# Tap matrices in runs of six pixels of one group, in two involution layers

## The chip, the cores and the metric

The kernel runs on one core of a Trainium2 chip. The metric is the device time of one execution in microseconds, the median over several runs. The core has five engines with instruction streams of their own: PE multiplies matrices and writes to PSUM, DVE and ACT read PSUM and SBUF, POOL reads SBUF alone, and SP issues DMA transfers. They wait for one another by semaphores. All arithmetic is in fp32.

## The reference

Four residual layers work on `x`, of 4 images with 256 channels of 56 x 56 pixels. Each layer normalises its input by groups of eight channels and adds its result to `x`. Layers 0 and 2 are involutions: every pixel has its own 7 x 7 filter for each of 16 groups of 16 channels, computed from the pixel's own channels.

```python
# layer 0; layer 2 has a batch norm and a relu after reduce_w, and another pair behind the sum
h = jnp.einsum('bchw,oc->bohw', xk, reduce_w) + reduce_b[None, :, None, None]
kern = jnp.einsum('bchw,oc->bohw', h, span_w) + span_b[None, :, None, None]
kern = kern.reshape(b, G, 1, K * K, Ho, Wo)
out = (kern * patches).sum(axis=3)
...
x = x + _L0_conv_ref(_gn(x), ...)     # involution
x = x + _L1_conv_ref(_gn(x), ...)     # two 3 x 3 convolutions
x = x + _L2_conv_ref(_gn(x), ...)     # involution
x = x + _L3_conv_ref(_gn(x), ...)     # gates from sums over a Fourier transform
```

`h` has 64 rows. `span_w` makes of it 49 filter taps for each group.

## The kernel before

The change touches layers 0 and 2 alone, which share the function `involution_layer`. The image is cut into tiles of 3 x 8 pixels (`TY`, `TX`; 24 pixels, `TP`). 19 x 7 tiles (`NT`, 133) cover it. The window that a tile needs, with the border of the filter, has 9 x 14 pixels (`Q`, 126): the partitions of one matmul. A column of tiles (`tx`, seven of them) is the unit of the apply work.

A unit of work is one image `b` and one half `cb` of the channels, eight groups (`GB`). There are eight units in each of the two layers, counted here 0 to 7 in layer 0 and 8 to 15 in layer 2. Each has two phases.

**Tap phase.** `tap_matrices` (L582) fills `kt`, for each group and each of a tile's 24 pixels the 126 x 133 matrix of what each window pixel counts for that pixel, over all tiles. One matmul (L593) gives one pixel of one group: the stationary operand is a stretch of 126 columns of the span table `z_sb`, which holds the 49 taps of a group spread over a field of `ZN` = 161 columns with zeros between them, shifted by the pixel's place; the moving operand is `hp`, the 64 rows of `h` at that pixel of every tile. Since only 64 rows are summed over, `hp` lies twice in SBUF, on partitions 0 to 63 and 64 to 127, and two matmuls run beside each other on the two halves of the array. The table has even groups on the first half of the partitions and odd groups on the second, so a step takes three pixels (`PB`) of two groups: six matmuls into two PSUM banks. Thirty-two steps make a unit. Every third step is evacuated by ACT with six activations that add the bias (L604), the others by DVE with one operation (L611). Other work (norms, window transposes, loads) is put between the steps by `hooks`.

The layout is `kt = [Q, GB, TP // PB, NT, PB]`: in one partition a group has eight blocks of three pixels, and in a block the three pixels of one tile lie beside each other.

**Apply phase.** For each column of tiles, `apply` (L623) multiplies the windows `xw` with the tap matrices. The stationary operand is a window with the channels of four groups (64) or two groups (32), the moving operand those groups' 24 pixels of that tile out of `kt` (L635): 96 or 48 elements, read in runs of `PB`. Two or four such matmuls run beside each other on column tiles of the array. A column has 20 matmuls of the first kind and 36 of the second. ACT and DVE then pick each channel's own group out of the four or two (L648 or L650, L655), and POOL (L660) or DVE (L662) adds the result to `x` in SBUF.

The windows come by a chain of their own: a strip of the normalised image (`strip_sb`, one buffer; L391 on POOL in layer 0, L389 on ACT in layer 2), seven transposes on PE (L406), a copy out of PSUM by ACT (L418) into one of three buffers `xw`, and four DMA transfers within SBUF that move rows between partitions (L424, L426, issued by SP, one of the four in layer 0 by POOL). This runs three columns ahead.

**Order.** Every engine runs its instructions in the order in which the program issues them (`in_order`). In the column loop of L1107 a column's apply is followed by `next_windows` and `next_strip`, the sums of the column before, and the closures in `late[tx]`: the next image's bottleneck, in layer 2 the gating of the image before (`next_load`, `next_gate` on POOL), and in unit 6 the building of the table for layer 2.

**The span tables.** Layer 0's is built at the start by ACT (`begin`, L496; `span_table`, L334). Layer 2's is built by POOL in the last image of layer 0 (`tables2`, L1004), stored to DRAM with one transfer (L1014), and loaded before unit 8 (L971). PSUM is used in four double banks (`two_banks`).

Of the kernel before, what the change touches and what calls it, by code (L numbers as in the profile page):

```python
# [16 lines left out]
P = 128  # L17
# [5 lines left out]
R = 64  # L23
# [19 lines left out]
ZN = ZF + Q  # L43
PB = 3
ROWS_H = 9
# [26 lines left out]
def net_kernel(  # L72
# [44 lines left out]

    z2_dram = dram.tile([P, G // 2, ZN], F32, name="z2_dram")
    zb2_dram = dram.tile([Q, G, TP], F32, name="zb2_dram")
# [179 lines left out]
    def involution_layer(layer, xin, xout, red, span, sb, xs_of, ahead=None, pending=None):  # L299

        with ExitStack() as es:
# [24 lines left out]
            if layer == 0:  # L326
# [3 lines left out]
                nc.scalar.activation(norm_sb[:, 3, B - 1, 1, :], mhalf, AF.Sigmoid)  # L330
            z_sb = wpool.tile([P, G // 2, ZN], F32, name="z_sb")
            zb_sb = wpool.tile([Q, G, TP], F32, name="zb_sb")

            def span_table(z_sb, span, scratch, load, copy):  # L334


                taps = scratch[:, : NB * KK * KK * GB].rearrange("p (cb k g) -> p cb k g", cb=NB, g=GB)
                for i in range(2):
                    for cb in range(NB):
                        load(taps[i * R : (i + 1) * R, cb], span[cb * R : (cb + 1) * R])  # L340
                nc.gpsimd.memset(z_sb, 0.0)
                yield
                for i in range(2):
                    half = slice(i * R, (i + 1) * R)
                    for cb in range(NB):
                        m = GB // 2
                        for gp in range(m):
                            copy(
                                field(z_sb[half, cb * m + gp, :]),
                                taps[half, cb, :, 2 * gp + i].rearrange("p (y x) -> p y x", x=KK),  # L350
                            )
                            yield
# [143 lines left out]
            def begin():  # L496
# [83 lines left out]
                return folds  # L580

            def tap_matrices(b, cb, hooks):  # L582

                hp = h_of[b]
                kt = big.tile([Q, GB, TP // PB, NT, PB], F32, name="kt")
                for n in range(GB // 2 * TP // PB):
                    gp, pb = divmod(n, TP // PB)
                    ps = two_banks()
                    for k in range(PB):
                        py, px = divmod(pb * PB + k, TX)  # L590
                        z0 = ZF - py * QX - px
                        for i in range(2):
                            nc.tensor.matmul(  # L593
                                ps[:Q, i, k * NT : (k + 1) * NT],
                                z_sb[i * R : (i + 1) * R, cb * GB // 2 + gp, z0 : z0 + Q],
                                hp[i * R : (i + 1) * R, py, px].rearrange("p a t -> p (a t)"),
                                start=True,
                                stop=True,
                            )
                    g0, p0 = 2 * gp, pb * PB  # L600
                    if n % 3 == 2:
                        for i in range(2):
                            for k in range(PB):
                                nc.scalar.activation(  # L604
                                    kt[:, g0 + i, pb, :, k],
                                    ps[:Q, i, k * NT : (k + 1) * NT],
                                    AF.Identity,
                                    bias=zb_sb[:, cb * GB + g0 + i, p0 + k : p0 + k + 1],
                                )
                    else:  # L610
                        nc.vector.tensor_tensor(  # L611
                            kt[:, g0 : g0 + 2, pb],
                            ps[:Q, :, : PB * NT].rearrange("q i (k t) -> q i t k", k=PB),
                            zb_sb[:, cb * GB + g0 : cb * GB + g0 + 2, p0 : p0 + PB]
                            .unsqueeze(2)
                            .to_broadcast([Q, 2, NT, PB]),
                            ALU.add,
                        )
                    for h in hooks.get(n, ()):
                        h()  # L620
                return kt
# [347 lines left out]
            else:  # L969
                since = mark()  # L970
                nc.sync.dma_start(z_sb, z2_dram)  # L971
                nc.sync.dma_start(zb_sb, zb2_dram)
# [31 lines left out]
            def tables2():  # L1004
# [6 lines left out]
                next(biases)  # L1011
                yield from span_table(z2, span2, scratch, nc.sync.dma_start, nc.gpsimd.tensor_copy)
                next(biases)
                nc.sync.dma_start(z2_dram, z2)  # L1014
                yield

            prev = None
            for u, (b, cb) in enumerate(units):
# [70 lines left out]
                if layer == 2 and b > 0:  # L1089
                    if cb == 0:  # L1090
                        late[0] += [lambda b=b, j=j: load_sf(b - 1, j) for j in range(2)]
                    for tx in range(1, 6) if cb == 0 else range(NTX - 2):
                        late[tx] += [next_load, next_gate]
                if last_image and cb == 0:
                    for tx in range(6):
# [663 lines left out]
```

## Time and profile before

| what | value |
|---|---|
| median of 3 runs | 1796.4 us (1794.46 to 1797.01) |
| span of the profiled execution | 1791.4 us |
| granted TensorE clock, mean | 0.985 |
| a tap phase, first to last matmul, units 0 to 7 | 23.9 to 27.4 us |
| a tap phase, units 8 to 15 | 26.2 to 30.2 us |
| apply phases of units 0, 2, 4 and 6, seven columns | 28 to 29 us |
| apply phases of units 9, 11 and 13 | 34 to 36 us |
| one apply column without other work | 4.11 us |
| layer 1, the convolutions | from 513 to 1257 us |

A line of the groups reads: line of the kernel, engine, operation, tile written <- tiles read, shapes, count | busy time in us, mean ns of one | idle time of the engine just before them, and what ended it. A fp32 matmul shows as two records[...]: how fast they run is read from how far apart they start. PEld is the loading of the stationary operand. In the timeline the columns are the start in us, the length in us, the engine, the line, the operation and how many of them were merged; a bracket is idle time before it and what ended it. The page's other parts add that DVE was busy 77% of the span and the DMA engines moved 120 GB/s on average, in the last third 150 to 220.

### The profile page before, as it was taken

To read this page: it belongs to the slowest core of one execution; us is meant where nothing else is said; L and a number is where in the kernel's file an instruction comes from. 1 tells how busy PE (TensorE), PEld (TensorE's weight loads), DVE (VectorE), ACT (ScalarE), POOL (GpSimd) and SP (SyncE) were. 2 spreads that over 40 slices of the span, in tenths; PEclk is the share of its full clock that TensorE was granted. 3 is DMA by queue.
4 is the path that set the end of the run, shared out by engine and by line. 5 is a ranking of instruction groups with operands and counts; after the bars stand their busy time and mean duration, and the time that the engine had idled before them with its cause. 6 is when DMAs were issued, how large, how long until landed. Compare 5 with 4: busy or idle time off the path is not lost.

```text
span 1791.4 us, 55774 instructions
## 1 busy us (share of the span) xinstructions
PE 1716.7 (96%) x24040; PEld 1507.5 (84%) x24040; DVE 1385.3 (77%) x2745; ACT 813.5 (45%) x1882; POOL 406.2 (23%) x627
## 2 busy tenths in 40 slices
PE   6999999999999999999999999999999999999998
PEld 4998988889978988898889888986888887788886
DVE  2777787767778988988898889885777778687775
ACT  2555556555533222222323132111767667567564
POOL 2224422444320000000000000001000355463572
PEclk9999999999989999999999999999999999999997
DMA  2445444633653021211111111122344567566653
GB/s 86 135 151 170 140 146 134 196 107 119 204 171 105 32 75 51 76 33 64 58 68 44 52 63 37 44 110 73 122 164 156 162 213 220 169 223 189 183 154 115
DMA packets 66003, 215.76 MB, mean 120 GB/s; under 512 B 13237, under 2 KB 20926, under 8 KB 62046
## 3 DMA queue, kind: packets, MB, share of 16 engines
q1 hardware_dynamic: 49262, 145.37, 25.9%
q0 software_dynamic: 14656, 64.77, 11.3%
q8 instruction: 190, 3.11, 0.7%
q10 hardware_dynamic: 1840, 2.05, 0.4%
q14 instruction: 55, 0.45, 0.1%
HBM read 76.30 MB, written 49.15 MB: 70 GB/s over the span
## 4 chain that ended last, share of the span: by engine, by line
PE 68%; DVE 19%; ACT 4%; DMA 4%; issue 3%; POOL 2%; SPq 1%; POOLq 0%; ACTq 0%; DVEq 0%
PE mm L1523 17%; PE ps L593 14%; PE ps L635 14%; PE mm L1441 9%; DVE kt L611 6%; PE mm L1412 5%; PE ps L406 3%; DMA xw<-xw 3%; DVE un L655 3%; PE ps L469 1%; DVE res L1516 1%; DVE xs L1375 1%; DVE st L1105 1%; ACT kt L604 1%; ACT hp L488 1%
## 5 line engine op out<-in xcount | busy, mean ns | idle before, releaser
L635 PE MATMUL ps<-kt,xw 126*32 126x48 f32 (+1 forms) x12544 | 381.8, 235 | 27.8 <-issue 12.2
L635 PEld LDWEIGHTS ps<-kt,xw 126*32 126x32 f32 (+1 forms) x12544 | 341.9, 121 | 74.5 <-issue 45.5
L593 PE MATMUL ps<-hp,z_sb 64*126 64x133 f32 x6144 | 383.2, 279 | 8.4 <-DVE kt L611 4.6
L1523 PE MATMUL mm<-v,u_sb 128*128 128x280 f32 (+1 forms) x1728 | 383.5, 383 | 1.9 <-DVE u_sb L1254 1.5
L593 PEld LDWEIGHTS ps<-hp,z_sb 64*126 64x126 f32 x6144 | 363.6, 185 | 24.4 <-DVE kt L611 6.8
L611 DVE TENSOR_TENSOR kt<-ps,zb_sb 126x798 f32<-126x798 f32 x352 | 332.9, 980 | 60.4 <-PE ps L593 49.2
L1523 PEld LDWEIGHTS mm<-v,u_sb 128*128 128x128 f32 x1728 | 326.1, 189 | 56.3 <-DVE u_sb L1254 1.9
L604 ACT ACTIVATE kt<-ps,zb_sb 126x133 f32<-126x133 f32 x960 | 280.1, 441 | 107.3 <-PE ps L593 107.3
L1441 PE MATMUL mm<-v,u_sb 128*128 128x252 f32 (+1 forms) x936 | 209.5, 384 | 0.0
L1441 PEld LDWEIGHTS mm<-v,u_sb 128*128 128x128 f32 x936 | 176.4, 189 | 30.5 <-issue 0.8
L655 DVE SCALAR_TENSOR_TENSOR un<-ps,s,un 128x240 f32<-128x240 f32 x224 | 102.6, 458 | 86.7 <-ACT un L650 79.9
L1560 POOL DMA_DIRECT2D x<-xs x24 | 13.1, 547 | 680.1 <-DVE xs L1559 426.5
L655 DVE SCALAR_TENSOR_TENSOR un<-ps,par_sb,un 128x240 f32<-128x240 f32 x224 | 98.1, 457 | 86.8 <-ACT un L648 82.3
L1508 ACT ACTIVATE res<-xs,shift,norm_sb 128x1120 f32<-128x1120 f32 (+1 forms) x24 | 30.2, 1258 | 236.3 <-DVE xs L1559 107.3
L418 ACT COPY xw<-ps 126x896 f32<-126x896 f32 x112 | 101.2, 905 | 44.0 <-PE ps L406 38.5
L406 PE MATMUL ps<-ident_sb,strip_sb 128*126 128x128 f32 x784 | 111.9, 283 | 8.4 <-POOL strip_sb L391 5.3
L660 POOL TENSOR_TENSOR xs<-un,xs 128x240 f32<-128x240 f32 x112 | 72.1, 664 | 192.2 <-DVE un L655 192.1
L648 ACT ACTIVATE un<-ps,par_sb 128x240 f32<-128x240 f32 x112 | 50.1, 448 | 122.5 <-PE ps L635 120.6
L650 ACT ACTIVATE un<-ps,bn_t,s 128x240 f32<-128x240 f32 x112 | 60.1, 537 | 94.7 <-PE ps L635 88.7
L406 PEld LDWEIGHTS ps<-ident_sb,strip_sb 128*126 128x126 f32 x784 | 85.1, 142 | 19.5 <-POOL strip_sb L391 8.3
L1412 PE MATMUL mm<-xs,u_sb 128*128 128x126 f32 (+1 forms) x792 | 98.7, 277 | 2.3 <-DVE xs L1375 1.3
L1412 PEld LDWEIGHTS mm<-xs,u_sb 128*128 128x128 f32 x792 | 94.4, 191 | 3.7 <-DVE xs L1428 1.6
(256 smaller groups left out, 1903.1 us busy)
## 6 DMA issues: line engine op xcount, KB each, us to landing
xw<-xw SPq DMA_DIRECT2D x168, 252.0 KB
xw<-xw SPq DMA_DIRECT2D x224, 126.0 KB
xw<-xw POOLq DMA_DIRECT2D x56, 252.0 KB, 4.6
xs<-x SPq DMA_DIRECT2D x24, 560.0 KB
x<-xs POOLq DMA_DIRECT2D x8, 1568.0 KB, 7.5
xs<-x SPq DMA_DIRECT2D x8, 1568.0 KB
xs<-in_x_dram SPq DMA_DIRECT2D x6, 1568.0 KB
x<-xs SPq DMA_DIRECT2D x6, 1568.0 KB
```

Of the source, the lines that this page charges most:

```text
L406: nc.tensor.transpose(ps[:Q, k * P : (k + 1) * P], flat[:, k * Q : (k + 1) * Q], ident_sb)
L418: nc.scalar.copy(xw[:, :NSB, :], ps[:Q, : NSB * P].rearrange("q (n c) -> q n c", n=NSB))
L593: nc.tensor.matmul(ps[:Q, i, k * NT : (k + 1) * NT], z_sb[i * R : (i + 1) * R, cb * GB // 2 + gp, z0 : z0 + Q], hp[i * R : (i + 1) * R, py ...
L604: nc.scalar.activation(kt[:, g0 + i, pb, :, k], ps[:Q, i, k * NT : (k + 1) * NT], AF.Identity, bias=zb_sb[:, cb * GB + g0 + i, p0 + k : p0 ...
L611: nc.vector.tensor_tensor(kt[:, g0 : g0 + 2, pb], ps[:Q, :, : PB * NT].rearrange("q i (k t) -> q i t k", k=PB), zb_sb[:, cb * GB + g0 : cb ...
L635: nc.tensor.matmul(v[m * j : m * j + m, i, :, k * TP : (k + 1) * TP], xw[:, window(ty), m * j : m * j + m], kt[:, ng * j : ng * j + ng, :, ...
L650: nc.scalar.activation(part, o[0], AF.Identity, bias=bn["t4"][:, cb : cb + 1], scale=bn["s4"][ng][:, 0, cb : cb + 1])
L655: nc.vector.scalar_tensor_tensor(part, o[e], s, part, ALU.mult, ALU.add)
L660: nc.gpsimd.tensor_tensor(dst, u, dst, ALU.add)
L1412: nc.tensor.matmul(ps[:, co * m : (co + 1) * m], u[ci][:, co * P : (co + 1) * P], v2[:, e, : n // 2, ci * WT : (ci + 1) * WT], start=(ci = ...
L1441: nc.tensor.matmul(ps, u1_sb[:, ci, dy, k, co * P : (co + 1) * P], v[:, k, dy * NB + ci : (dy + n - 1) * NB + ci + 1 : NB, :], start=(j == 0),
L1523: nc.tensor.matmul(ps, u2_sb[:, ci, dy, k, co * P : (co + 1) * P], v[:, k, dy * NB + ci : (dy + n - 1) * NB + ci + 1 : NB, :], start=(j == 0),
```

## The change

A step of the tap phase makes six pixels of one group instead of three pixels of two groups. Both halves of the array now work on the same group, the first on pixels 0 to 2 of the six, the second on 3 to 5. So `kt` becomes `[Q, GB, 4, NT, 6]`, with the six pixels of a tile beside each other, and each group's table has to lie on both halves of the partitions. There are as many steps, matmuls, activations and DVE operations as before, with the same numbers of elements.

In layer 0 the table gets twice the columns (16 groups on all 128 partitions). In layer 2 it keeps its size and holds the eight groups of one `cb` at a time: it is loaded again for each unit, in the second column of the unit before. The stored table has all groups on both halves, written with eight transfers.

```diff
-PB = 3
+PB, PR = 6, 3
...
-    z2_dram = dram.tile([P, G // 2, ZN], F32, name="z2_dram")
+    z2_dram = dram.tile([NB, P, GB, ZN], F32, name="z2_dram")
...
-            z_sb = wpool.tile([P, G // 2, ZN], F32, name="z_sb")
+            z_sb = wpool.tile([P, G if layer == 0 else GB, ZN], F32, name="z_sb")
...
-            def span_table(z_sb, span, scratch, load, copy):
+            def span_table(z_sb, span, scratch, load, copy, halves=((slice(0, P), 1),)):
...
-                for i in range(2):
-                    half = slice(i * R, (i + 1) * R)
+                for half, by in halves:
                     for cb in range(NB):
-                        m = GB // 2
-                        for gp in range(m):
+                        m = GB // by
+                        for g in range(m):
                             copy(
-                                field(z_sb[half, cb * m + gp, :]),
-                                taps[half, cb, :, 2 * gp + i].rearrange("p (y x) -> p y x", x=KK),
+                                field(z_sb[half, cb * m + g, :]),
+                                taps[half, cb, :, by * g + half.start // R].rearrange("p (y x) -> p y x", x=KK),
                             )
...
+            def load_taps(cb):
+                nc.sync.dma_start(z_sb, z2_dram[cb])
...
-                for n in range(GB // 2 * TP // PB):
-                    gp, pb = divmod(n, TP // PB)
+                for n in range(GB * TP // PB):
+                    g, pb = divmod(n, TP // PB)
                     ps = two_banks()
-                    for k in range(PB):
-                        py, px = divmod(pb * PB + k, TX)
-                        z0 = ZF - py * QX - px
+                    for k in range(PR):
                         for i in range(2):
+                            py, px = divmod(pb * PB + i * PR + k, TX)
+                            z0 = ZF - py * QX - px
                             nc.tensor.matmul(
                                 ps[:Q, i, k * NT : (k + 1) * NT],
-                                z_sb[i * R : (i + 1) * R, cb * GB // 2 + gp, z0 : z0 + Q],
+                                z_sb[i * R : (i + 1) * R, cb * GB + g if layer == 0 else g, z0 : z0 + Q],
                                 hp[i * R : (i + 1) * R, py, px].rearrange("p a t -> p (a t)"),
...
-                    g0, p0 = 2 * gp, pb * PB
+                    zb = zb_sb[:, cb * GB + g, pb * PB : (pb + 1) * PB]
                     if n % 3 == 2:
                         for i in range(2):
-                            for k in range(PB):
+                            for k in range(PR):
+                                p = i * PR + k
                                 nc.scalar.activation(
-                                    kt[:, g0 + i, pb, :, k],
+                                    kt[:, g, pb, :, p],
...
                         nc.vector.tensor_tensor(
-                            kt[:, g0 : g0 + 2, pb],
-                            ps[:Q, :, : PB * NT].rearrange("q i (k t) -> q i t k", k=PB),
-                            zb_sb[:, cb * GB + g0 : cb * GB + g0 + 2, p0 : p0 + PB]
-                            .unsqueeze(2)
-                            .to_broadcast([Q, 2, NT, PB]),
+                            kt[:, g, pb].rearrange("q t (i k) -> q t i k", i=2),
+                            ps[:Q, :, : PR * NT].rearrange("q i (k t) -> q t i k", k=PR),
+                            zb.rearrange("q (i k) -> q i k", i=2).unsqueeze(1).to_broadcast([Q, NT, 2, PR]),
                             ALU.add,
...
-                nc.sync.dma_start(z_sb, z2_dram)
+                load_taps(0)
...
-                yield from span_table(z2, span2, scratch, nc.sync.dma_start, nc.gpsimd.tensor_copy)
+                halves = ((slice(0, R), 2), (slice(R, P), 2))
+                yield from span_table(z2, span2, scratch, nc.sync.dma_start, nc.gpsimd.tensor_copy, halves)
                 next(biases)
-                nc.sync.dma_start(z2_dram, z2)
+                for i in range(2):
+                    by = z2[i * R : (i + 1) * R].rearrange("r (cb g) z -> r cb g z", cb=NB)
+                    for h in range(2):
+                        to = z2_dram[:, h * R : (h + 1) * R].rearrange("cb r (g i) z -> r cb g i z", i=2)
+                        for c in range(NB):
+                            nc.sync.dma_start(to[:, c, :, i], by[:, c])
...
+                if layer == 2 and u + 1 < len(units):
+                    late[1].append(lambda cb=cb: load_taps(1 - cb))
```

## The prediction

> **What bounds the kernel now.** I read the page first, then the groups with shapes kept apart, then the chain and the timeline of one tap phase and of a few columns. PE is busy nearly all the span, so what is looked for is time in which PE is slow, not idle.
>
> ```profile
> PE 1716.7 (96%) x24040; PEld 1507.5 (84%) x24040; DVE 1385.3 (77%) x2745; ACT 813.5 (45%) x1882; POOL 406.2 (23%) x627
> ```
> ```profile
> L635 PE MATMUL ps<-kt,xw 126*64 126x96 f32 x4480 | 256.6, 266 | 15.2 <-DMA xw<-xw 11.7 <-DVE un L655 2.0
> L635 PE MATMUL ps<-kt,xw 126*32 126x48 f32 x8064 | 134.5, 218 | 12.6 <-issue 12.2
> ...
> L1320 ACT ACTIVATE ph<-xs,norm_sb 128x294 f32<-128x294 f32 x32 | 27.2, 918 | 1.8 <-POOL xs L660 1.8
> ```
> The apply matmuls (L635) hold PE for 391 us: 112 columns of 112 records, two records to each fp32 matmul. They read `kt` in pieces of three floats. What a record would cost without such pieces is read from the chain, where convolutions and tap matmuls run back to back:
>
> ```profile
> 175.60 13.67 PE ps L593 x228
> ...
> 630.34 15.30 PE mm L1441 x72
> 645.64 33.96 PE mm L1523 x144
> ```
> 252 columns take 15.30/72 = 212.5 ns and 280 take 33.96/144 = 235.8 ns: 0.833 ns a column plus 2.5. These two read runs of 14 floats, so a break in the run is not what costs. The taps (133 columns in one run, two half arrays side by side) come to 13.67/228 x 2 = 120 ns, where the rule gives 113. The apply records should then take 82.5 ns (96 columns) and 42.5 ns (48). The timeline of a column says otherwise:
>
> ```profile
> 199.37 1.99 PEld L635 LDWEIGHTS ps<-kt,xw 126*64 126x64 f32 x40 [0.17 <-issue]
> 201.53 0.99 PEld L635 LDWEIGHTS ps<-kt,xw 126*32 126x32 f32 x72 [0.16 <-issue]
> 202.60 0.98 PE L406 MATMUL ps<-ident_sb,strip_sb 128*126 128x128 f32 x7
> ```
> Forty records, two tiles abreast, fill 199.37 to 201.53 less a changeover of 0.16: 20 rounds of 100 ns. Seventy-two, four abreast, fill 201.53 to 202.60 less about 0.15: 18 rounds of 51 ns. The excess is 17.5 ns for 32 runs of three and 9 ns for 16 runs: 0.55 ns a run in both. Tiling of the array is not its source, for two column tiles with 56 columns in one run keep the rule's 49 ns; one tile's records start 50 ns apart:
>
> ```profile
> 1404.70 0.21 PE L764 MATMUL ps<-cs_sb,m 56*56 56x56 f32 x1
> ...
> 1404.75 0.21 PE L764 MATMUL ps<-cs_sb,m 56*56 56x56 f32 x1
> ...
> 1404.80 0.21 PE L764 MATMUL ps<-cs_sb,m 56*56 56x56 f32 x1
> ```
> The tap phase has a second limit close by:
>
> ```profile
> 180.19 1.75 ACT L604 ACTIVATE kt<-ps,zb_sb 126x133 f32<-126x133 f32 x6 [0.30 <-PE ps L593]
> 180.95 1.88 DVE L611 TENSOR_TENSOR kt<-ps,zb_sb 126x798 f32<-126x798 f32 x2 [0.24 <-PE ps L593]
> 182.32 1.76 ACT L604 ACTIVATE kt<-ps,zb_sb 126x133 f32<-126x133 f32 x6 [0.37 <-PE ps L593]
> ```
> Three steps take 2.05 to 2.12 us, PE's own 3 x 0.68; DVE works 1.88 of them and ACT 1.75. And in layer 0 the strip on POOL comes only just in time for the transposes:
>
> ```profile
> 203.76 1.29 POOL L660 TENSOR_TENSOR xs<-un,xs 128x240 f32<-128x240 f32 x2 [1.40 <-DVE un L655]
> ...
> 205.58 0.90 POOL L391 TENSOR_SCALAR strip_sb<-xs,norm_sb 128x616 f32<-128x616 f32 x1
> ...
> 206.71 0.99 PE L406 MATMUL ps<-ident_sb,strip_sb 128*126 128x128 f32 x7
> ```
>
> **What the Trainium skill says.** "SBUF — State Buffer", Specifications (TRN2), gives 16-byte lines and says that at least two hits on a line are needed for full rate. Runs of 12 bytes at every alignment leave a single hit in half of their cases; 24-byte runs on steps of 24 bytes split 4+2 or 2+4, never with a single one, as the 56-byte runs of the convolutions do. The 0.55 ns a run and the convolutions' nothing agree. "DMA: Bandwidth & Descriptors", Issuing engines are not separate DMA queues, has all queues' transfers on the same 16 engines; so the new loads of `z_sb` share them with the `xw` moves. "TensorEngine Tiling (Array Packing)", Key Properties, says that a change of tiling mode drains the array: the 0.16 to 0.17 us before each part, which stay.
>
> **The change part by part.** (1) Apply reads runs of six. I take the whole excess as gone: 20 x 17.5 + 18 x 9 = 512 ns of a column's 3.27 us of matmuls. Bounds: nothing, and 512; half is what a cost per run, however long, would give, which the runs of 14 speak against.
>
> What of it reaches the end. In layer 0 a steady column takes 4.11 us (transposes at 202.60 and 206.71). The strip that POOL ends at 206.48 hangs, through ACT, DVE and L660, on the matmuls that began the last of their rounds at 202.46: with its semaphore some 4.12 us, whatever PE does. PE's own path falls to 3.60 us, 3.45 of it from one column's transposes to the last round of the next; two columns then take 3.45 + 4.12, so 3.78 each: 0.33 saved, not 0.51. A unit with `cb` 0 gains about 2.4 us (0.5 for its first column, nothing for the next, 0.33 or so for five); the three with the bottleneck, where ACT's and DVE's turns leave PE waiting, 2 each; the last, held by the convolution's loads, 1. Layer 0: 4 x 2.4 + 3 x 2 + 1 = 16.6. In layer 2 units 9, 11 and 13 have PE busy 94 to 99% and I give them 2.5 of 3.6 each; unit 8, where DVE's 3.5 us a column is next, 2; units 10, 12, 14 and 15, in which DMA engines are busy 66 to 78% and PE waits for `xw` already, 0.8 each. Sum 12.7.
>
> (2) Tap phase, PE: 32 steps of six matmuls as before, same 133-column reads, same 126-column loads. Nothing.
>
> (3) Evacuation by DVE: 798 elements as before; the inner step in PSUM stays 133 floats, and the half index moves inside it, to another bank. 980 ns either way; no row shows a read that changes bank every third element, so the bounds are -5% (longer runs of bias) and +20%. It stays hidden to +0.17 us in two steps.
>
> (4) Evacuation by ACT: writes at steps of 24 bytes, not 12. Six in 1.75 us, the last lasting 0.44, are 0.26 us apart, no more than 133 elements at 0.83 and a start-up of 0.15, so the present step costs no rate. PE allows 2.05/6 = 0.342. The nearest row for a lone element per line is the 16-byte-step read of L1320: (918 - 351)/294 = 1.93 ns an element, 351 being what L650's 551 ns leave after 240 elements at 0.833. If writes overlap the next start-up, 133 x 1.93 = 0.257 us, hidden; if they do not, 0.257 + 0.143 = 0.40. I take the first, as the 12-byte writes already show no cost.
>
> (5) `load_taps`: seven more loads of 644 KB on SP, behind the second column's `xw` moves; SP issues one in 0.42 us and its four `xw` moves in 3.3, of a 3.6 us column. The transfer takes 2 to 3 us of the engines, and `xw` moves queue behind it. With the column 0.5 shorter, their slack of some 1.5 us at the fourth column is mostly used up: 1 us lost in each of four `cb` 0 units (bounds 0 and 2.5), nothing beside the 5.8 us columns of `cb` 1. Cost 4.
>
> (6) Eight stores of the table for one: issued at 457 us, at 0.6 us each they hold SP to about 463, and what follows is wanted at 490. The copies that fill it are as many as before, on POOL. The doubled memset (1.2 us more on POOL at 4 us) ends long before POOL's next turn at 25. ACT's 16 table copies span all rows and stay 16. Nothing.
>
> Sum: -16.6 - 12.7 + 4 = -25. The profiled span of 1791.4 becomes 1766; the median of the runs, 1796.4, lies 5.0 above the span, so 1771.5, say 1772.
>
> **The rivals.** A: the short runs are dear for another reason (three nested dimensions, say) and six cures half: 0.26 a column, of which POOL's limit hides nothing, 29 on PE but some 10 after waits and loads: 1786. For it: both penalties fit a price per run. Against: L1441 and L1523. B: the gain is real and is eaten, columns being ended by `xw` landings and POOL: the source of L635's waits shows 18.8 us of DMA now. Gain 8 to 10 less 7 to 10 for loads: 1796. Against: units 9, 11, 13 are bound by PE. C, slower: ACT's writes at one element a line. Place: the 84 or so groups of three steps which run at 2.05 to 2.12 us now (the others have 0.7 us to spare). It decides from 0.342 us an activation, and beats the gain of 25 from 0.342 + 25/(84 x 6) = 0.39. At 0.40 it costs 84 x 6 x 0.058 = 29: net 1800. For it: L1320. Against: the 12-byte writes run at full rate. A DVE that takes 20% more costs alike.
>
> **How the numbers follow.** Forecast 0.53 (its own range 1761 to 1783), A 0.13, B 0.12, C 0.22. No change means within 0.2%, 3.6 us, about what a measurement of this kernel can tell. Faster: 0.53, 0.11 of A and 0.02 of B, 0.66. Same: 0.02 of A, 0.08 of B, 0.02 of C, 0.12. Slower: 0.02 of B, 0.20 of C, 0.22. The range 1762 to 1804 leaves about 0.06 below and 0.11 above.
>
> **What would show it.** Right: the 40 loads of a column's first part in some 1.65 us, the 72 in about 0.8; layer 0 columns 3.75 to 3.8 apart with PE waiting for `strip_sb`; L593, L611 and the tap phases as before; six ACT evictions within 2.05. Wrong: the same 1.99 and 0.99 (step 1), six evictions over 2.05 us with PE waiting for `kt` L608 (step 4), DVE's 980 ns grown (step 3), or PE waits for `xw` beyond 25 us in layer 2 (step 5).

## The result, and the profile after

The changed kernel takes 1798.8 us, median of 20 runs (1792.0 to 1807.9), against 1796.4 us for the kernel before (20 runs): ratio 1.0018, 95% interval 1.0005 to 1.0030. The forecast was 1772. PE does work less; the page of the changed kernel, busy us of each engine with its share of the span:

```profile
PE 1682.8 (94%) x24040; PEld 1469.8 (82%) x24040; DVE 1387.3 (77%) x2745; ACT 822.8 (46%) x1882; POOL 406.8 (23%) x627
```

PE's busy time falls by 34 us and the span by 1.2 (1791.4 to 1790.2): the work went, the time stayed as idle PE. The profiled execution is moreover the quickest of the 20 (1791.96 us), so a typical one lost more than this trace shows. The groups of the changed kernel with shapes kept apart (busy us, mean ns of one | idle time before them and what ended most of it) say where:

```profile
L637 PE MATMUL ps<-kt,xw 126*64 126x96 f32 x4480 | 228.9, 251 | 16.7 <-DMA xw<-xw 10.6 <-DVE un L657 3.5 <-issue 1.1
L637 PE MATMUL ps<-kt,xw 126*32 126x48 f32 x8064 | 120.8, 207 | 36.6 <-issue 36.4
...
L615 DVE TENSOR_TENSOR kt<-ps,zb_sb 126x798 f32<-126x798 f32 x352 | 332.8, 980 | 63.8 <-PE ps L596 63.2
...
L608 ACT ACTIVATE kt<-ps,zb_sb 126x133 f32<-126x133 f32 x960 | 290.1, 492 | 101.0 <-PE ps L596 101.0
```

The apply matmuls (L635 before, L637 now) hold PE for 41 us less (256.6 + 134.5 to 228.9 + 120.8). Start to start, as a median over the columns, a round of the 96-column ones goes from 100 to 86 ns and of the 48-column ones from 52 to 44. A column's matmuls go from 3.27 to 2.83 us (before, then after):

```profile
203.51 3.27 PE L635 MATMUL ps<-kt,xw 126*64 126x96 f32 x112
```
```profile
206.68 2.83 PE L637 MATMUL ps<-kt,xw 126*64 126x96 f32 x112
```

Beside it stands the bill: "issue" ahead of the 48-column matmuls was 12.2 us and is 36.4, idle time in which PE waits on no semaphore.

By stage, from each unit's first and last matmul: units 0 to 7 gain 10.6 us in their columns, lose 2.4 in their tap phases, and the start of this execution was 1.1 us late. At the end of unit 7 the changed kernel is 6.5 us ahead, at the end of unit 13 still 6.2, at the end of unit 15 only 0.7. Layer 2 returns all that layer 0 brought. Its waits of PE in the two kernels (engine, line, what it waited for: us in total, times, longest), before:

```profile
PE ps L635 <- issue: 9.7, 15, 1.3
PE ps L635 <- DMA xw<-xw: 8.9, 8, 2.2
```

and after:

```profile
PE ps L637 <- issue: 29.4, 25, 3.8
PE ps L637 <- DMA xw<-xw: 9.6, 10, 2.8
```

The longest of these stops, in unit 10, as PE's timeline shows it:

```profile
1418.66 1.96 PE L637 MATMUL ps<-kt,xw 126*64 126x96 f32 x55 [0.20 <-DMA xw<-xw]
1424.42 0.77 PE L637 MATMUL ps<-kt,xw 126*32 126x48 f32 x49 [3.81 <-issue]
1425.12 1.75 PE L405 MATMUL ps<-ident_sb,strip_sb 128*126 128x128 f32 x7
1426.80 3.73 PE L637 MATMUL ps<-kt,xw 126*64 126x96 f32 x112
```

PE stops in the middle of a column at 1420.62, and no semaphore wait is shown. The DMA part of the profile for the 3.8 us of the stop (queue, kind: packets, MB, share of the 16 engines):

```profile
q0 software_dynamic: 161, 0.58, 50.6%
q1 hardware_dynamic: 188, 0.47, 41.1%
q8 instruction: 1, 0.02, 2.0%
```

The engines are 94% busy with the window moves that queued up behind the load of taps (its packets started from 1414.8 to 1420.0) and gating's chunks (q1, q0), and one packet of 16 KB, kind "instruction", gets through, from 1421.81 to 1423.00; 1.4 us later PE goes on. Queue 8 carries 190 such packets in an execution: 65 bytes for each of the 48,080 records of PE and PEld, so it is read here as PE's program. There are 20 stops over 0.4 us without a wait in layer 2, 28.1 us in all, where before there were ten, 8.2 us. All 20 end 1.2 to 1.7 us after such a packet has landed, and so do all ten before (1.3 to 1.5 us). With one packet every 6 us that is no accident. The nine longest (1.3 us and more, 19.5 us) are those whose packet landed after PE had stopped, or at most 0.2 us before. PE running out of program, because the packets that bring it stand in line, fits all of this; no run changed the program's own traffic, so it is argued from the times. What then follows is in the windows of the same place (us; PE, PEld, DVE, ACT, POOL busy; granted clock, DMA share, GB/s):

```profile
1421.00:1424.00 3.00, 0.00 (x0) 0.00 (x0) 1.67 (x4) 0.00 (x0) 0.69 (x2) 1.00 0.92 284
1424.00:1425.00 1.00, 0.58 (x49) 0.57 (x48) 0.00 (x0) 0.00 (x0) 0.00 (x0) 0.99 0.95 245
1425.00:1428.00 3.00, 2.93 (x34) 2.23 (x23) 1.34 (x3) 1.61 (x3) 0.57 (x2) 0.50 0.86 272
```

From 1425.0 the granted clock is 0.50 for 3.4 us; the transposes (L405), 0.98 us before, take 1.75. Layer 2's units have four such stretches after, one before. The Trainium skill, "TensorE: Matmul & The Clock Gate", What's actually happening, says that the array's clock is halved after an idle window of about 3.4 us, in free-running windows. The 3.4 us and the half agree; the window need not be wholly idle, for the three between 1684 and 1743 us follow 2.2 to 2.8 us of idle PE.

In layer 0 the second limit of the forecast is there. POOL's timeline of two steady columns after:

```profile
202.97 1.30 POOL L662 TENSOR_TENSOR xs<-un,xs 128x240 f32<-128x240 f32 x2 [1.12 <-DVE un L657]
204.22 0.55 POOL L425 DMA_DIRECT2D xw<-xw  x1
204.82 0.89 POOL L390 TENSOR_SCALAR strip_sb<-xs,norm_sb 128x616 f32<-128x616 f32 x1
206.90 1.30 POOL L662 TENSOR_TENSOR xs<-un,xs 128x240 f32<-128x240 f32 x2 [1.19 <-DVE un L657]
208.14 0.55 POOL L425 DMA_DIRECT2D xw<-xw  x1
208.74 0.89 POOL L390 TENSOR_SCALAR strip_sb<-xs,norm_sb 128x616 f32<-128x616 f32 x1
```

The transposes follow the strip at once (205.76 and 209.68): a column takes 3.92 us, where 4.11 stood before and 3.78 was forecast, and the group of transposes between 60 and 500 us shows what PE waits for (5.3 us before):

```profile
L405 PE MATMUL ps<-ident_sb,strip_sb 128*126 128x128 f32 x371 | 52.3, 281 | 13.4 <-POOL strip_sb L390 10.5 <-issue 2.1
```

### The profile page after: what moved, and what is told of

The parts are those of the page before. It is cut to its first block, busy times and chain, and to the rows that moved or that the text cites. A ratio compares the mean times of both kernels' runs of the same rounds, so it can differ in the third digit from the quotient of the medians.

```text
span 1790.2 us, 55795 instructions
## 1 busy us (share of the span) xinstructions
PE 1682.8 (94%) x24040; PEld 1469.8 (82%) x24040; DVE 1387.3 (77%) x2745; ACT 822.8 (46%) x1882; POOL 406.8 (23%) x627
## 4 chain that ended last, share of the span: by engine, by line
PE 64%; DVE 20%; ACT 5%; issue 4%; DMA 4%; POOL 2%; SPq 1%; POOLq 0%; ACTq 0%; DVEq 0%
PE mm L1533 18%; PE ps L596 15%; PE ps L637 9%; PE mm L1451 9%; DVE kt L615 5%; PE mm L1422 5%; DVE un L657 4%; DMA xw<-xw 3%; PE ps L405 2%; PE ps L468 1%; ACT kt L608 1%; DVE st L1115 1%; DVE res L1526 1%; POOL strip_sb L390 1%; DVE xs L1385 1%
## 5 line engine op out<-in xcount | busy, mean ns | idle before, releaser
L596 PE MATMUL ps<-hp,z_sb 64*126 64x133 f32 x6144 | 387.6, 280 | 8.4 <-DVE kt L615 4.2
L637 PE MATMUL ps<-kt,xw 126*32 126x48 f32 (+1 forms) x12544 | 340.4, 223 | 53.3 <-issue 37.5
L637 PEld LDWEIGHTS ps<-kt,xw 126*32 126x32 f32 (+1 forms) x12544 | 302.7, 118 | 99.4 <-issue 71.2
L608 ACT ACTIVATE kt<-ps,zb_sb 126x133 f32<-126x133 f32 x960 | 290.1, 492 | 101.0 <-PE ps L596 101.0
L405 PE MATMUL ps<-ident_sb,strip_sb 128*126 128x128 f32 x784 | 113.2, 286 | 16.4 <-POOL strip_sb L390 10.5
L405 PEld LDWEIGHTS ps<-ident_sb,strip_sb 128*126 128x126 f32 x784 | 86.0, 143 | 28.0 <-POOL strip_sb L390 17.9
```

The costliest lines, as they stand in the source:

```text
L405: nc.tensor.transpose(ps[:Q, k * P : (k + 1) * P], flat[:, k * Q : (k + 1) * Q], ident_sb)
L596: nc.tensor.matmul(ps[:Q, i, k * NT : (k + 1) * NT], z_sb[i * R : (i + 1) * R, cb * GB + g if layer == 0 else g, z0 : z0 + Q], hp[i * R : ...
L608: nc.scalar.activation(kt[:, g, pb, :, p], ps[:Q, i, k * NT : (k + 1) * NT], AF.Identity, bias=zb[:, p : p + 1],)
L637: nc.tensor.matmul(v[m * j : m * j + m, i, :, k * TP : (k + 1) * TP], xw[:, window(ty), m * j : m * j + m], kt[:, ng * j : ng * j + ng, :, ...
```

## The experiments

Ratios are to the kernel before, on the same chip, with 95% intervals; 0.1% is 1.8 us.

### Which part costs: table, loads, layers

`packed6` keeps the old table (two groups a step, no loads of taps) and takes the new `kt` alone; a step fills half of a run of six.

```diff
-PB = 3
+PB, PR = 6, 3
...
-                for n in range(GB // 2 * TP // PB):
-                    gp, pb = divmod(n, TP // PB)
+                for n in range(GB // 2 * TP // PR):
+                    gp, pb = divmod(n, TP // PR)
+                    run, at = divmod(pb * PR, PB)
...
-                            kt[:, g0 : g0 + 2, pb],
+                            kt[:, g0 : g0 + 2, run, :, at : at + PR],
```

> The old table (two groups a step, three pixels each, no loads of taps in layer 2) with the new kt of runs of six, each step filling half of a run. Theory LOADS (the seven 644 KB loads of taps delay, on the shared DMA engines, the transfers that bring PE its program in layer 2; the trace after has PE gaps of over 0.4 us without a wait of 28.2 us in layer 2 against 8.2 before): these gaps fall back to 8 to 12 us, one half-clock stretch of 3.4 us in layer 2 instead of four, and the time is 1781 to 1788. Theory PACE (columns that are 0.5 us shorter ask for their program sooner than layer 2's other traffic lets it arrive; the loads don't matter): gaps stay above 20 us, time within 4 us of the changed kernel's, 1794 to 1801.

`before_loads` is the kernel before with loads alone:

```diff
+                if layer == 2 and u + 1 < len(units):
+                    late[1].append(lambda: nc.sync.dma_start(z_sb, z2_dram))
```

> The kernel before, with its z_sb of layer 2 loaded again (the same data, 644 KB) in each of layer 2's units but the last, at the place where the changed kernel loads its taps. LOADS: slower by 5 to 9 us (1801 to 1806), gaps without a wait in layer 2 at 15 to 28 us. PACE: within 2 us of before, gaps 7 to 12 us.

`layer0_only` and `layer2_only` hold both versions of `tap_matrices` and the table that each needs:

```diff
+            tap_matrices = tap_new if layer in (0,) else tap_old
```

> The change in layer 0 alone, layer 2 as before. Both theories: layer 0's 6.5 us of gain stay, layer 2 costs nothing: 1788 to 1791. If the start (1.1 us later in the trace after) and the tap phases are paid in layer 0 in a typical run as in the profiled one, not below 1787; a time within 2 us of before would say that the profiled run flattered layer 0.

> The change in layer 2 alone, layer 0 as before. Both theories: the shorter columns are worth nothing there and the gaps and half-clock stretches cost 5 to 10 us: 1800 to 1806, gaps without a wait in layer 2 at 20 us or more. Below 1796 would say that the profiled run of the changed kernel misled about layer 2.

| kernel | ratio | interval | median us |
|---|---|---|---|
| changed | 1.0018 | 1.0005 to 1.0030 | 1798.8 |
| packed6 | 0.9935 | 0.9919 to 0.9951 | 1781.2 |
| before_loads | 1.0080 | 1.0058 to 1.0101 | 1808.7 |
| layer0_only | 0.9960 | 0.9944 to 0.9976 | 1785.2 |
| layer2_only | 1.0078 | 1.0054 to 1.0103 | 1806.0 |

LOADS holds in the times, and more strongly than it was put: the loads cost the old columns 0.80% (14 us), where 5 to 9 were expected, and what parts the changed kernel from `packed6` is 0.83%. In `packed6`'s layer 2 the stops without a wait are half of the changed kernel's:

```profile
PE ps L636 <- issue: 15.4, 21, 2.4
PE ps L636 <- DMA xw<-xw: 9.8, 10, 1.8
```

and in `before_loads`, whose columns are the old ones, both kinds of wait are up (9.7 and 8.9 before):

```profile
PE ps L635 <- issue: 16.7, 14, 2.2
PE ps L635 <- DMA xw<-xw: 14.6, 14, 3.0
```

with six half-clock stretches in its units of layer 2 where the kernel before has one. The stops of `packed6` (14.6 us over 0.4 us each) did not fall to the 8 to 12 us expected, so the quicker columns add some of their own; its half-clock stretches did go, from four to none. Each of these traces is one execution, `packed6`'s the quickest of its 22.

The loads' price is not spread evenly over the seven. By columns against the kernel before, the units of `before_loads` with `cb` 0 (8, 10, 12 and 14) are 2.8, 3.5, 2.5 and 6.0 us longer, units 9, 11 and 13 only 0.0, 0.4 and 1.3.

`layer0_only` is at -0.40%, 7 us: layer 0 gains less than half of what was forecast for it. `packed6` stands only 0.25% (5 us, with some 4 either way) below it, so layer 2's shorter columns, free of loads, seem to bring less than their 12.7 as well. Beside the loads they bring nothing that these runs can tell: `layer2_only`, with shorter columns and loads, is at 1.0078, and `before_loads`, with loads alone, at 1.0080.

### Is it the bytes, the burst or the queue

`after_spread` cuts each load in four, behind columns 1 to 4; `after_actq` lets ACT issue it; `before_half_loads` is `before_loads` with half the bytes.

```diff
-                    late[1].append(lambda cb=cb: load_taps(1 - cb))
+                    for k in range(4):
+                        late[1 + k].append(lambda cb=cb, k=k: load_part(1 - cb, k))
```

> The changed kernel, each load of taps in four pieces of two groups (161 KB) behind columns 1 to 4 in place of one of 644 KB behind column 1. Theory BURST (a load stands in the DMA queues ahead of the windows' moves and of PE's program for as long as it is large): gaps without a wait in layer 2 fall to 8 to 15 us, the time to 1786 to 1792 (ratio 0.995 to 0.998). Rival BYTES (the 644 KB come on top of traffic that the columns leave no room for, wherever they are): as the changed kernel, ratio 1.000 to 1.004, gaps 20 us or more.

> The changed kernel with its seven loads of taps issued by ACT in place of SP, at the same place. If what matters of a load is that it stands in SP's queue ahead of the windows' moves, this gives back as much as the four pieces did or more: ratio 0.995 to 0.999, waits for the moves down. If it is the load's packets on the shared DMA engines, whichever queue they come by, ratio 1.000 to 1.004 and gaps without a wait in layer 2 of 20 us or more.

```diff
-                    late[1].append(lambda: nc.sync.dma_start(z_sb, z2_dram))
+                    late[1].append(lambda: nc.sync.dma_start(z_sb[:, :4], z2_dram[:, :4]))
```

> The kernel before with loads of half the table (322 KB) where before_loads has 644 KB. BYTES: half of its 0.8%, so a ratio of 1.003 to 1.005. A price per load, whatever its size: 1.007 to 1.009. A threshold (half the load fits in what the columns leave free): 0.999 to 1.002.

Half the bytes cost half: 1.0039 (1.0025 to 1.0054). Four pieces give 0.9986 (0.9971 to 1.0001), between the two expectations: 0.3% of the loads' 0.8% came from the burst, the rest stays with the same bytes in small pieces. ACT's queue is no relief, 1.0059 (1.0031 to 1.0088). Its layer 2 waits, in an execution 11 us quicker than its median:

```profile
PE ps L640 <- DMA xw<-xw: 24.9, 14, 3.8
PE ps L640 <- issue: 13.9, 19, 2.2
```

Against 9.6 and 29.4 in the changed kernel: in this pair of traces the load takes its share from the window moves in place of the program. The sum of the two is the same 39 us. The Trainium skill, "DMA: Bandwidth & Descriptors", Issuing engines are not separate DMA queues, says that transfers of all queues run on the same 16 engines and interleave; this run agrees, and suggests that the queue decides who is made to wait.

### Gating's traffic

Three kernels without the gating of the first three images in layer 2:

```diff
-                            chunks.extend(gate_chunk(pb, j, c) for j in range(NCHUNK) for c in range(NB))
+                            pass
...
-                        late[0] += [lambda b=b, j=j: load_sf(b - 1, j) for j in range(2)]
+                        pass
```

> The changed kernel without the gating of the first three images in layer 2: their chunks are neither loaded again, nor computed, nor written to the output, and the gate maps aren't loaded (84 transfers of 224 KB and 21 broadcast ones less). If the loads of taps cost because they meet this traffic, gaps without a wait in layer 2 fall from 28 to below 8 us, and the time is within 4 us of packed6 without gating. If they cost by themselves, it stays 8 us or more above it.

> packed6 without the same gating, as the partner of the run before: with gating it is 0.8% below the changed kernel (15 us). Below packed6 with gating by 0 to 10 us, since what stays of its gaps without a wait (14.5 us in layer 2 of its trace) and of its waits for the moves is owed to gating too.

> The kernel before without the gating of the first three images (left out as in the two runs before: not loaded again, not computed, not written). If gating's traffic is what eats the gain of shorter columns in layer 2, the difference to packed6_nogate (0.9763) is larger than the 0.65% between packed6 and before: 1.1 to 1.5%, so a ratio of 0.987 to 0.991. If layer 2's shorter columns are worth 5 us in any case, 0.65%: ratio 0.982 to 0.984.

Without gating the changed kernel is at 0.9844 (0.9818 to 0.9870), packed6 at 0.9763 (0.9735 to 0.9792), the kernel before at 0.9869 (0.9837 to 0.9901). Two things follow. The loads still cost 0.81% (with an error of some 0.4 from the two intervals), so they don't need gating to hurt; the expectation that they would fade fell. The units that pay are plain here too, by their columns against `packed6_nogate`: units 8, 10, 12 and 14 are 3.6, 1.6, 4.6 and 2.6 us longer, units 9, 11 and 13 at most 0.4. In those three the next image's bottleneck makes the columns long, which probably hides the load. The clock is not what costs here: there is one half-clock stretch in layer 2 with the loads and none without, and unit 12 loses its 4.6 us at full clock. And the new `kt` brings 1.06% (19 us) here, where it brings 0.65% (12) beside gating. The two differ by no more than their intervals allow, and the profiled executions don't show it in layer 2, where `packed6` is 12.2 us shorter than the old kernel beside gating and 10.6 without; so that gating's traffic takes a part of the gain is not shown. PE's waits in layer 2 put both into three lines each; the kernel before:

```profile
PE ps L635 <- DVE un L655: 1.2, 3, 0.4
PE ps L635 <- DMA xw<-xw: 1.0, 1, 1.0
...
PE ps L635 <- issue: 0.7, 1, 0.7
```

packed6:

```profile
PE ps L636 <- DMA xw<-xw: 5.1, 5, 1.8
PE ps L636 <- DVE un L656: 3.6, 6, 0.8
...
PE ps L636 <- issue: 2.2, 5, 0.6
```

the changed kernel:

```profile
PE ps L637 <- DMA xw<-xw: 8.9, 10, 1.7
PE ps L637 <- issue: 8.6, 10, 1.8
PE ps L637 <- DVE un L657: 3.6, 6, 0.8
```

Each step, quicker columns and then loads, leaves PE waiting longer for windows and stopping longer without a wait, at a DMA share of 0.5 to 0.6 in the columns of units 10, 12 and 14; with gating (0.6 to 0.86) the same steps start higher.

### ACT's writes

`layer2_only` has both forms in one execution, L609 in the new layout and L648 in the old:

```profile
L609 ACT ACTIVATE kt<-ps,zb_sb 126x133 f32<-126x133 f32 x480 | 144.9, 492 | 53.2 <-PE ps L597 53.2
...
L648 ACT ACTIVATE kt<-ps,zb_sb 126x133 f32<-126x133 f32 x480 | 140.5, 441 | 51.1 <-PE ps L637 51.1
```

An activation lasts 51 ns longer on steps of 24 bytes, while they start 0.26 us apart as before. Six take 1.81 us for 1.75, and a steady tap phase takes 24.25 us for 23.92 (units 2, 4, 6), in `packed6` as in the changed kernel. That it is so because the pair of PSUM banks comes free later is argued. Longer steps come with `PB = 12` and `PB = 24` in packed6's form:

> The old table, kt in runs of twelve, so that an activation of ACT writes single pixels on steps of 48 bytes and apply reads runs of 48. Theory TAIL (an activation's end grows with the step of its writes: 441 ns on 12-byte steps, 492 on 24; it frees its PSUM pair later and the tap phases pay): 530 to 590 ns, and a steady tap phase of 24.5 to 24.8 us against 24.25. Rival WRITES (492 ns is the price of any step over 16 bytes): 492 ns, 24.25 us. For apply: that runs of six left nothing, rounds stay at 85 and 43 ns and the time is 0 to 6 us over packed6; if they left something, rounds of 82 and 42 and up to 7 us less.

> The same with runs of 24 pixels: a group's taps of one place lie in one piece, ACT writes on steps of 96 bytes. TAIL: 580 to 800 ns, tap phases of 24.8 us and more, the time 4 to 15 us over packed6. WRITES: 492 ns, tap phases as packed6, time within 3 us of it or up to 7 less if apply gains.

With 48-byte steps ACT is as with 24, with 96 it is slower (packed12, then packed24):

```profile
L605 ACT ACTIVATE kt<-ps,zb_sb 126x133 f32<-126x133 f32 x960 | 289.0, 489 | 105.0 <-PE ps L594 105.0
```
```profile
L605 ACT ACTIVATE kt<-ps,zb_sb 126x133 f32<-126x133 f32 x960 | 344.3, 609 | 79.0 <-PE ps L594 78.8
```

DVE's evacuation goes on average from 987 to 1043 ns in both. The times are 0.9954 (0.9937 to 0.9971) and 1.0112 (1.0090 to 1.0134): twelve is not told apart from six; with 24 six activations take 2.23 us and a steady tap phase 26.3, 2.0 more than packed6's. WRITES fits up to 48 bytes and TAIL at 96; neither fits both, and the reason for the step between them stays open.

Apply did gain once more: rounds are 83 and 43 ns with runs of twelve and of 24, and a column's matmuls go from 2.84 to 2.77 us (packed6, then packed12). That is 8 us of PE over the 112 columns, which the times don't show.

```profile
205.45 2.84 PE L636 MATMUL ps<-kt,xw 126*64 126x96 f32 x112
```
```profile
207.51 2.77 PE L636 MATMUL ps<-kt,xw 126*64 126x96 f32 x112
```

### Layer 0's strip

Three ways to have the strip sooner, all on packed6. `packed6_actstrip`:

```diff
-                if layer == 2 and len(strips) > 2:
+                if len(strips) > (2 if layer == 2 else 4):
```

> packed6 with layer 0's strips written by ACT in place of POOL, as layer 2's are. Theory STRIP (in layer 0 a column waits for the strip that POOL writes behind its two additions, which kept the gain at 1.2 to 1.5 us a unit where 2.4 was forecast): layer 0's units of channel block 0 get 0.8 to 1.5 us shorter, the wait for strip_sb falls from over 10 us to below 3, and the time is 5 to 10 us below packed6's 0.9935 of before. Rival: ACT's 1.05 us for a strip delays its evacuations, PE waits for those in place of the strip, and the time is as packed6's or above.

`packed6_strip_first`:

```diff
-                        nc.gpsimd.tensor_tensor(dst, u, dst, ALU.add)
+                        add = lambda dst=dst, u=u: nc.gpsimd.tensor_tensor(dst, u, dst, ALU.add)
+                        if y0 < H:
+                            add()
+                        else:
+                            behind.append(add)
...
                     next_strip()
+                    if behind:
+                        behind.pop()()
```

> packed6 with layer 0's strip ahead of a column's second addition on POOL, in place of behind it (every operation stays on its engine). Theory STRIP: the wait for strip_sb in layer 0 falls from 11.5 us to below 3, steady columns of channel block 0 fall from 3.94 us to 3.6 to 3.7, and the time is 6 to 10 us below packed6's: ratio to before 0.988 to 0.990. Rival SHORT: PE meets another wait at about the same point (its program, the column's evacuations), columns 3.85 us or more, ratio 0.992 to 0.995.

`packed6_spmove`:

```diff
-                    eng = nc.sync if layer == 2 or j == 1 else nc.gpsimd
+                    eng = nc.sync
```

> packed6 with the fourth move of a window set in layer 0 issued by SP, as in layer 2, in place of POOL. If POOL's string of additions, the move's issue (0.55 us) and the strip is what holds layer 0's columns at 3.94 us, they fall to 3.65 to 3.75, the wait for strip_sb to below 5 us, and the ratio to before is 0.987 to 0.991. If another wait takes its place (SP's fourth issue of 0.8 us, so later windows, or PE's program), columns of 3.85 us or more and a ratio of 0.992 to 0.997.

They come to 0.9912 (0.9888 to 0.9937), 0.9953 (0.9938 to 0.9968) and 0.9903 (0.9873 to 0.9932), packed6 being at 0.9935 (0.9919 to 0.9951). With the strip first the wait for it falls from 11.5 us only to 7.0, for POOL's issue of the window move still stands ahead of it and itself waits, for ACT's copy:

```profile
207.11 0.71 POOL L663 TENSOR_TENSOR xs<-un,xs 128x240 f32<-128x240 f32 x1 [0.64 <-DVE un L658]
...
208.21 0.55 POOL L426 DMA_DIRECT2D xw<-xw  x1 [0.40 <-ACT xw L418]
208.81 0.90 POOL L391 TENSOR_SCALAR strip_sb<-xs,norm_sb 128x616 f32<-128x616 f32 x1
209.67 0.62 POOL L663 TENSOR_TENSOR xs<-un,xs 128x208 f32<-128x208 f32 x1
```

The column at this place takes 3.82 us, in packed6 3.94, but the last addition of a unit is now late and the tap phase behind it, up to the first apply matmul, is 0.7 us longer (25.80 for 25.10): nothing is won. With the move on SP the wait is 4.2 us, and nine of the twenty steady columns of units 0, 2, 4 and 6 take 3.61 to 3.76 us, about what was expected, the others up to 5.06. From the first tap matmul to the end of unit 7 this kernel takes 455.5 us, where packed6 takes 464.5, the changed kernel 460.8 and the kernel before 468.4, in one profiled execution each. With the strip on ACT the wait for it is gone, and PE's stops without a wait between 60 and 500 us grow from 6.1 to 12.2 in the profiled execution, the slowest of its six. Both ratios are below packed6's (SP by 0.32%, ACT by 0.23%), but the intervals overlap, so whether either beats packed6 is not settled; both, and packed6, beat the kernel before and the changed one.

## Why the prediction was wrong

The trace of the kernel before was read rightly as to what PE loses and wrongly as to who else was near the limit. Of the 28 us between the forecast and the result, some 10 are the loads (5), some 10 what layer 0 keeps and some 8 what layer 2 keeps of the shorter columns (1).

(1) Apply, on PE: nearly right. 440 ns a column went, of 512 forecast, and rival A's half cure (256) is out. What reaches the end in layer 0: forecast 16.6 us, measured 7 (`layer0_only`, 4.3 to 10); in the trace of the changed kernel it is 10.6 in the columns less 2.4 in the tap phases. The units with the bottleneck were put nearly right, 1.5, 2.1 and 1.5 us for 2 each, and the last, 0.9 for 1. The four with channel block 0 gain 0.7 to 1.5 us in their columns, for 2.4: the alternation of two paths, 3.45 and 4.12, was to give 3.78 a column and gave 3.92. The strip's string on POOL includes the issue of a window move, 0.55 us. `packed6_spmove` takes it away, and in its profiled execution layer 0's units take 12.9 us less than before. In layer 2: forecast 12.7, some 5 without loads beside gating (the difference of `packed6` and `layer0_only`, with some 4 either way). The units where PE waits for windows had been given a little; that PE's program travels with the same traffic was not seen. The profiled executions put the gain without loads nearer to the forecast: from the end of unit 7 to that of unit 15 `packed6` is 12.2 us shorter than the kernel before, and 10.6 with gating away in both. One execution each doesn't settle which holds.

(2) Tap matmuls, nothing: right; 280 ns a record for 279, and `packed6`, whose steps take their operands as before, has the same tap phases.

(3) DVE's evacuation, nothing: right, 980 ns in both.

(4) ACT's evacuation, hidden: the rate was right (0.26 us apart, far from the 0.342 at which rival C begins), the working left out the end of the last activation. The tap phases are 0.33 us longer where steady and 2.4 us over layer 0's eight. The 1.93 ns an element that was taken from L1320 rests on a start-up borrowed from another line; L1320's own rows (294, 280 and 266 elements in 918, 895 and 876 ns) give 1.5. Rival C's place was right; its price, 29 us, needed a rate that the writes don't have up to 48-byte steps (0.324 us apart at 96).

(5) The loads of taps, 4 us: this is the step that failed most. They cost 14, shown three times: on the old columns (0.80%), on the new (0.83%, changed kernel against packed6), and without gating (0.81%). It was priced as 1 us of used-up slack in each of the four units with `cb` 0, and nothing in the others. Where the cost falls was right, its size was not: those four pay 12.4 us together without gating and 14.8 in `before_loads`, so 3.1 to 3.7 each, beyond the bound of 2.5. A load's 644 KB, at the 284 GB/s that the engines moved in the stop shown, are 2.3 us, and its packets took 5.2 us to start among the others; so these units lose more than its bytes' time, not what exceeds a slack. Half the bytes at half the price speaks for bytes and against a price per load. What the working left out, as far as the times tell, is the traffic that brings PE its program: from `packed6` to the changed kernel PE's stops without a wait in layer 2 grow by 14.0 us (15.4 to 29.4), its waits for `xw` not at all (9.8 to 9.6).

(6) Stores, memset and copies: nothing, right as far as runs tell. The eight stores take 1.4 us each to issue, not 0.6, and with the next moves they hold SP from 451.2 to 466.1 us; nothing is late; the start that was 1.1 us late in the trace after is 0.3 us early in `layer0_only`, which has the same start.

With -7 for layer 0, ACT's part in it, -5 for layer 2's columns and +14 for the loads, the sum is +2, and +3 was measured. The -5 is itself a difference of two of these kernels, so this closes nearly by construction; what was measured apart is the -7 and the 14. Rival B, the gain eaten by landings and POOL, named the end (1796) and the kind of cause, but with some luck: its gain of 8 to 10 (12 in `packed6`) and its price for the loads, 7 to 10, were both too low. The waits for landings that it rested on hardly grew (8.9 to 9.6 in layer 2), and the 18.8 us that it read for them add the idle time of PEld to that of PE, which alone had 11.7. The wait that the forecast set as its mark for step 5, over 25 us for `xw`, did not appear (9.6): in the changed kernel the loads showed as stops without any wait, while in `before_loads` both kinds grew.

## What to carry to other kernels

Before adding a load to a stage, read its DMA share and PE's idle time without a wait, and don't price it by the slack of one consumer. Here a load cost about 3 us in each unit with short columns, more than its bytes' time, at a mean DMA share of 0.5 to 0.6 as at 0.6 to 0.86. Moving it to ACT's queue did not make it cheaper; beside the long columns of the bottleneck it cost little. A layout gain doesn't need the table that came with it: writing half runs from the old steps gave the quicker reads, and 12 us, without one byte more. And when a busy engine is relieved, the next limit may be in another engine's order of issues, even a DMA issue of half a microsecond ahead of the work that is waited for.

## What the runs showed of the hardware

- PE's program seems to come over the same DMA engines, in packets of 16 KB (190 in an execution, about 1.1 us each in layer 2), and a busy stage delays it: all 20 stops over 0.4 us without a wait in the changed kernel's layer 2 end 1.2 to 1.7 us after such a packet has landed, and all ten before 1.3 to 1.5 us after one. That the packet ends the stop is read from these times; no run changed the program's own traffic.
- A stop can cost twice. From unit 0 to the end of unit 15, in all 17 traces, every stretch of 3.4 us of the clock's own grid with more than 1.95 us of idle PE (59 of them) was followed by 3.4 us at a granted clock of 0.50; it needs no wholly idle stretch. Between 1.5 and 1.95 some were and some were not. The mean granted clock, as a median over runs, is 0.984 for the kernel before, 0.979 for the changed one, 0.978 for `layer2_only`.
- PE's reads of 96 columns take 100 ns a round in runs of three, 86 in runs of six and 83 in runs of twelve and of 24, beside the 82.5 worked out from the convolutions' runs of 14. The groups' totals hide the last step (226.3 us in packed6, 228.7 and 228.2 with twelve and 24), for they include what runs at half clock: no such stretch in packed6's layer 2, seven and six in the others.
- An activation with single-element writes lasts 441, 492, 489 and 609 ns for steps of 12, 24, 48 and 96 bytes.
